# A two-layer convolution and attention kernel: folded rows in the spectra of x, packed scores, an edge row of its own, and scalings moved around the attention of layer 0

## The chip, the cores and the metric

The kernel runs on one core of a Trainium2 chip. The metric is the device time of one execution in microseconds, from the start of the program to the end of its last engine. Four compute engines work beside each other, each through its own list of instructions in order: PE (TensorE, matrix products, writes to PSUM), DVE (VectorE), ACT (ScalarE) and POOL (GpSimd). SP (SyncE) issues most DMAs.

## The reference, cut to what matters

The input `x` is 4 batches x 32 channels x 128 x 128 in float32. Layer 0 is a Fourier layer with attention over the 32 channels ("images" here), layer 1 a causal additive attention and a mixture of experts. The change touches layer 0 only.

```python
def _L0_conv_ref(x, ...):
    xn = _inorm(x.reshape(B * T, 1, H, W), norm1_w, norm1_b)
    k = _fno_layer(xn, Kcw, Ksw, Hs, Ws)      # 32 heads, at 64 x 64
    q = _fno_layer(xn, Qcw, Qsw, Hs, Ws)
    v = _fno_layer(xn, Vcw, Vsw, H, W)
    scores = jnp.einsum('bntk,bnsk->bnts', qf, kf) / sqrt(Hs * Ws)
    p_attn = softmax(scores)
    av = jnp.einsum('bnts,bnsk->bntk', p_attn, vf)
    p = _fno_layer(av, Pcw, Psw, H, W)
    a = _inorm(p + xa, attn_w, attn_b)
    an = _inorm(a, norm2_w, norm2_b)
    m = _fno_layer(an, m0cw, m0sw, H, W, inner_norm=True, act=True)
    m = _fno_layer(m, m1cw, m1sw, H, W, inner_norm=True, act=False)
    return _inorm(m, mon_w, mon_b) + a

x = x + _L0_conv_ref(_gn(x), ...)             # _gn: normed in 32 groups of columns
t = _to_tokens(x)
t = t + _L1_attn_ref(_ln_t(t), ...)
t = t + _L1_ffn_ref(_ln_t(t), ...)
```

`_fno_layer` multiplies the low Fourier modes of an image by learnt weights and adds the image times a scalar. The scores are therefore sums over modes: for keys and queries 32 rows (kx) and 17 columns (ky) carry weights for each head, all other modes of the 64 x 33 half spectrum only the scalars.

## The kernel before

**Batches and hand-overs.** Layer 0 goes through the four batches in one Python loop (`for b in range(B)`, L784), layer 1 follows. In the loop, batch `b` is mixed (attention), goes through its two mask convolutions, and near the end of its pass the spectra and the attention weights of batch `b + 1` are computed (`spectra_of_images`, `attention_weights`), so that three hand-overs stand between four batches; for batch 0 both run ahead of the loop (L696, L740). In layer 0 a scheduler sets each engine's order by the program's order and by the data; `behind(later, earlier)` adds an order by hand without a wait.

**Spectra of images** (L457 to L504). Per group of 8 images: `first_step` (L268) multiplies each image (as weights, 128 x 128) by the 128 columns `rows`, the cosines and sines of 64 kx, into `pz`. ACT copies `pz` to `z` and writes the negative of the first half behind it (L277, L278), two DVE instructions add the group's mean at kx = 0 (`shift`, L470). `forward` (L280) then makes two matmuls per image, weights `z[:, k, :P]` and `z[:, k, 64:]`, with 67 columns of `colg`, into `px` (L287, L288). DVE scales `px` by the image's inverse deviation `ysc` into `xx` (L480): partitions are (re or im, kx), columns ky. Eight DMAs write `xx` to `xd` in DRAM (L492).

**Attention weights** (L541 to L652). `xx` is copied to `xe` and `xm` (ky ahead of images) and `xe` to `xp` in PSUM. The modes without head weights (ky 17 to 32) go by matmuls into `so` (L569, 16 of them in one column group). Then 17 turns over ky: DVE and POOL multiply shifted image pairs into `pa` and `pb` (L582, L584; six buffers of tag `pr`), PE weighs them by head into `sp` and `sp0` (L597, L599). `sod` (DVE, L587) spreads `so`. ACT copies `sp` to `spt` (L601), short matmuls add all up in `sc` (L608 to L618), then maximum, difference, exponential `ex` on ACT (L625), sum, reciprocal, and `ph` on POOL (L633). `ph` goes through DRAM (`prd`, L645) into `pr` (L649), the weights of the mixing.

**Beside it, in a hand-over, batch b ends**: `spectra(1, gl, early)` (L950) makes the spectrum of the second mask convolution; `weighed` (L996) sums its energies into `v1` and `vc`, and from these some 20 small DVE steps and two pairs of Ln and Exp on ACT give the coefficients `c2`, `c3`, `cq` (L1119 to L1141). ACT scales the 32 images (`scale`, L1148), POOL adds them to `xr` in four pieces (`add_scaled`, L1158), and `back` (L339) transforms back: PE `y` (`row_products`, L321), ACT copy `v` (L335), PE `four` (L337), DVE update `last` (L1177), in two halves of 16 images. Between the halves `skip_matrix` (L654: `cm`, `cd`, `cp`, `bd`) makes the mixing matrix of the skip path. The four results go out to `x1` (L1200).

**Mixing** (L832 to L878). In blocks of 13 kx rows and 4 groups of 8 images: SP loads `xb` from `xd`, repeated over 16 heads (L841, four buffers), ACT copies it to PSUM (`xw`, L850), POOL and DVE multiply by the value weights `gb` into `u` (L859, L861), and PE sums over images with `pr` into `po` (L798); ACT copies `po` to `rs` (L878).

**Ahead of the loop**: `value_weights` (L506) computes `gd`, writes it to DRAM and reads it back as `gb`, four DMAs of 1056 KB (L531); L700 to L732 make the score weights `w_re`, `w_im` and `qk`.

## Time and profile before

| | us |
|---|---|
| median of 3 runs | 2987.97 |
| lowest and highest | 2984.72, 2988.0 |
| the profiled execution | 2987.02 |
| its span (first to last instruction) | 2985.2 |
| up to the first `po` of batch 0 | 92.4 |
| first `po` of batches 1, 2, 3 | 304.01, 510.66, 712.62 |
| layer 0 ends, layer 1's loop starts | 898 |

Busy shares over the span: PE 93%, DVE 75%, ACT 78%, POOL 69%. They are means over stages with different limits: layer 1 takes 2087 of the 2985 us, and its stretch alone has PE at 1995.9 us busy. In the hand-over from 424 to 512 us PE is busy for 80.8 us, DVE 67.9, ACT 44.2 and POOL 34.5, with DMA at 22%; in the first 93 us PE 63.2, DVE 49.9, ACT and POOL 21.0 each, with DMA at 52%. So a stage has to be read by its own chain of waits, not by the totals. A line of a timeline gives start, length, engine, line of the kernel, operation, what is written and read, and how many; in brackets, how long the engine was idle before it and what ended that. A float32 matmul appears as two records.

### The profile page before, as it was taken

Reading aid. Unit: us, or ns where it says so; the run is one execution under the profiler, and the core shown is the slowest. Engines: PE = TensorE matmul, PEld = TensorE weight load, DVE = VectorE, ACT = ScalarE, POOL = GpSimd, SP = SyncE. Lnnn points to the kernel's source line nnn. Section 1 sums busy time; section 2 is a strip of 40 time slices with the busy share of each in tenths; the row PEclk is TensorE's granted clock in tenths of the full one; section 3 lists DMA queues with packets and bytes.
Section 4 is the critical chain, followed back from the end, with each engine's and each line's share of the span. In section 5 each row is a group of like instructions: output and inputs, shape, how many; then the busy total and the mean of one; then the engine's idle time right before and its main releaser. Section 6 shows DMA issues by size and latency. Waiting matters only on the chain.

```text
span 2985.2 us, 52875 instructions
## 1 busy us (share of the span) xinstructions
PE 2779.6 (93%) x19530; PEld 1385.4 (46%) x19530; DVE 2228.6 (75%) x5024; ACT 2317.5 (78%) x3173; POOL 2057.0 (69%) x1825
## 2 busy tenths in 40 slices
PE   7789899998878999999899999999999999999997
PEld 5366565674643444443444344444444444444443
DVE  5787788788876677775678688666778766877877
ACT  2545554455358999999999999989999998999992
POOL 1704605507407897878987978898787889798773
PEclk9899999999989999999999999999999999999998
DMA  5401403304112101001010100111010020100000
GB/s 132 148 10 39 147 1 88 98 10 126 38 33 61 33 1 40 8 8 45 20 26 15 25 15 8 34 32 33 15 25 15 8 52 17 29 11 23 15 15 15
DMA packets 151731, 112.91 MB, mean 38 GB/s; under 512 B 36046, under 2 KB 139825, under 8 KB 150833
## 3 DMA queue, kind: packets, MB, share of 16 engines
q1 hardware_dynamic: 148209, 107.44, 13.6%
q8 instruction: 154, 2.52, 0.4%
q10 hardware_dynamic: 3264, 2.10, 0.2%
q14 instruction: 104, 0.85, 0.1%
HBM read 68.53 MB, written 20.00 MB: 30 GB/s over the span
## 4 chain that ended last, share of the span: by engine, by line
PE 57%; POOL 14%; ACT 10%; DVE 9%; issue 6%; DMA 1%; POOLq 0%; SPq 0%; DVEq 0%; ACTq 0%
PE d L1632 19%; PE po L1651 11%; PE px L1538 6%; ACT r L1682 5%; PE n L1632 3%; POOL e L1691 3%; POOL e L1690 3%; POOL u L859 3%; PE po L798 2%; ACT e L1698 2%; DVE r L1687 2%; POOL kx L1297 2%; POOL x L1297 1%; PE sp L597 1%; PE pz L265 1%
## 5 line engine op out<-in xcount | busy, mean ns | idle before, releaser
L1687 DVE TENSOR_TENSOR r<-n,r 128x1024 f32<-128x1024 f32 (+1 forms) x1056 | 962.0, 953 | 479.7 <-PE n L1632 390.2
L1690 POOL TENSOR_TENSOR e<-r 128x512 f32<-128x512 f32 x528 | 674.0, 1277 | 267.6 <-DVE r L1687 267.0
L1682 ACT ACTIVATE r<-d 128x1024 f32<-128x1024 f32 (+1 forms) x1056 | 793.4, 803 | 62.4 <-PE n L1632 56.1
L1694 ACT ACTIVATE r<-r 128x1536 f32<-128x1536 f32 x528 | 783.7, 1484 | 16.7
L1691 POOL TENSOR_TENSOR e<-e,r 128x512 f32<-128x512 f32 x528 | 672.3, 1273 | 41.4
L1632 PE MATMUL d<-qe,ke 32*128 32x512 f32 (+3 forms) x2304 | 605.7, 602 | 41.7 <-ACT r L1682 37.6
L1651 PE MATMUL po<-e,kx 128*128 128x512 f32 (+3 forms) x1152 | 594.3, 605 | 15.8 <-POOL e L1703 15.8
L1632 PE MATMUL n<-qe,ke 32*128 32x512 f32 (+3 forms) x2304 | 606.2, 601 | 0.0
L1632 PE MATMUL n<-qf,kf 32*128 32x512 f32 (+3 forms) x2304 | 552.6, 554 | 0.0
L1632 PE MATMUL d<-qf,kf 32*128 32x512 f32 (+3 forms) x2304 | 550.1, 553 | 0.0
L1542 DVE SCALAR_TENSOR_TENSOR xc<-px,wgt,xc 128x128 f32<-128x128 f32 x1024 | 358.3, 350 | 43.1 <-PE px L1538 10.5
L1698 ACT ACTIVATE e<-e 128x512 f32<-128x512 f32 x528 | 326.0, 617 | 67.4 <-POOL e L1691 66.6
L1651 PEld LDWEIGHTS po<-e,kx 128*128 128x128 f32 x1152 | 175.4, 188 | 393.1 <-issue 306.9
L1632 PEld LDWEIGHTS d<-qe,ke 32*128 32x128 f32 x2304 | 176.5, 183 | 361.5 <-ACT r L1682 341.0
L1632 PEld LDWEIGHTS d<-qf,kf 32*128 32x128 f32 x2304 | 220.0, 186 | 176.6 <-issue 164.2
L1538 PE MATMUL px<-we,x2t 128*128 128x512 f32 x512 | 265.9, 605 | 7.0 <-DVE xc L1542 5.8
L859 POOL TENSOR_TENSOR u<-xb,gb 128x858 f32<-128x858 f32 (+1 forms) x112 | 220.8, 2008 | 49.9 <-PE po L798 44.7
L1632 PEld LDWEIGHTS n<-qf,kf 32*128 32x128 f32 x2304 | 228.3, 185 | 18.6 <-issue 11.5
L861 DVE TENSOR_TENSOR u<-xw,gb 128x858 f32<-128x858 f32 (+1 forms) x208 | 215.7, 1109 | 20.6 <-PE po L798 9.1
L986 POOL TENSOR_TENSOR spec<-part,part 128x512 f32<-128x512 f32 x16 | 24.9, 1556 | 283.9 <-DVE part L983 130.8
L798 PE MATMUL po<-u,pr 128*32 128x429 f32 (+1 forms) x1280 | 150.5, 534 | 37.5 <-POOL u L859 21.6
L1632 PEld LDWEIGHTS n<-qe,ke 32*128 32x128 f32 x2304 | 177.8, 183 | 9.3 <-DVE r L1687 0.9
(399 smaller groups left out, 3581.0 us busy)
## 6 DMA issues: line engine op xcount, KB each, us to landing
xb<-xd SPq DMA_DIRECT2D x128, 214.5 KB
xc<-x SPq DMA_DIRECT2D x29, 512.0 KB
x<-x SPq DMA_DIRECT2D x16, 512.0 KB
qf<-qe SPq DMA_DIRECT2D x64, 128.0 KB
out<-xc SPq DMA_DIRECT2D x15, 512.0 KB
x<-in_x SPq DMA_DIRECT2D x14, 512.0 KB
xb<-xd SPq DMA_DIRECT2D x32, 198.0 KB
gb<-gd SPq DMA_DIRECT2D x4, 1056.0 KB
```

What stands on the lines that cost most here:

```text
L859: nc.gpsimd.tensor_tensor(u, xb, gk, ALU.mult)
L861: weighed_last = nc.vector.tensor_tensor(u, xw, gk, ALU.mult)
L1538: nc.tensor.matmul(px, x2t[:, k * P : (k + 1) * P], we[:, e0 : e0 + 4], start=True, stop=True)
L1542: nc.vector.scalar_tensor_tensor(xc[:, k], px[:, e], wgt[:, k, e0 + e : e0 + e + 1], xc[:, k], ALU.mult, ALU.add)
L1632: nc.tensor.matmul(o, k, q, start=turn == 0 or g > 0, stop=turn == 1 or g > 0)
L1651: nc.tensor.matmul(sums[c, h][:, q0 : q0 + c1 - c0], kx[:, jb], e[:, c0:c1], start=jb == 0, stop=is_last and q0 > 2 * P, skip_group_check= ...
L1682: nc.scalar.activation(r[:, g], d, AF.Ln, scale=1.0 / DSCALE)
L1687: nc.vector.tensor_tensor(r[:, g], part, r[:, g], ALU.mult)
L1690: nc.gpsimd.tensor_tensor(e, r[:, 1], r[:, 2], ALU.add)
L1691: nc.gpsimd.tensor_tensor(e, e, r[:, 0], ALU.add)
L1694: nc.scalar.activation(r, r, AF.Exp, scale=-1.0)
L1698: nc.scalar.activation(e, e, AF.Exp)
```

## The change

**Folded rows.** `half_rows` takes 33 cosine and 33 sine columns instead of 128 (x is real, so rows kx and -kx follow from the same two sums). The 32nd column of both goes to a small tile `z32`, the rest to `z`, 64 numbers an image; the mean is added by one ACT instruction a group. Two images at a time are the weights of one matmul with 68 columns (`columns_of`, `it`), copied to `fold` by ACT. `unfold`, once per half of the images, turns the folded sums into rows by matmuls with tables of zeros and plus or minus ones (`of_cos`, `of_sin`) on 64 partitions: one set into `em`, already in the layout of the packed scores, one set into `std`, which becomes `xx`. DVE scales both out of PSUM; ACT copies the first half of `xe` once more behind it.

**Edge row.** Row kx = 32 is computed apart (`edge_row`) and has a 65th slot in `xd`; the other rows are stored turned by 32, `xb` is read from slot 1, and the copies of `po` to `rs` turn back (one of the five is cut in two). Some DMAs change size: `kq_raw` 1088 to 576 KB, `cst` 549 to 758 KB; `xd` is written by eight DMAs after each half of the images and one for the edge row, and those for batch 0 stand ahead of three of the four `gb` loads.

**Packed attention.** The weighted modes lie on all 128 partitions, so there are 9 turns instead of 17. `so` gets 34 matmuls in four column groups, 18 of them with `hm`, a copy of `xx` masked by ACT; `sod` and `qk` have 128 partitions.

**Energies by halves.** `energy` is called for the first four slots inside `spectra(1, ...)`, for the others in `coefficients`; `weighed` takes the sums. In the hand-overs `coefficients` runs from inside `spectra_of_images`.

**Scalings around attention.** Three hooks place ACT's `scale` and POOL's `add_scaled`: 16 and two ahead of `spt`, 8 and one between `spt` and `ex`, 8 after `ex`, the last addition after `ph`. POOL's `u` is put behind that addition.

```diff
+    def half_rows(images, z, last):
+
+        for k in range(0, GI, 4):
+            pz = ps.tile([P, 4, 2, KY], F32, name="pz", tag="a")
+            for j in range(4):
+                mm = nc.tensor.matmul(
+                    pz[:, j],
+                    images[k + j],
+                    rows.rearrange("p (r x) -> p r x", r=2)[:, :, :KY],
+                    start=True,
+                    stop=True,
+                )
+            nc.scalar.copy(z[:, k : k + 4], pz[:, :, :, :32])
+            nc.scalar.copy(last[:, :, k : k + 4], pz[:, :, :, 32].rearrange("p t r -> p r t"))
+        return mm
+
...
-        steps = []
-                z = grp.tile([P, GI, 192], F32, name="z", tag="z")
-                first_step([xt[:, g + t] for t in range(GI)], z, nc.scalar.copy)
-                for k in range(2):
-                    nc.vector.tensor_scalar(
-                        z[:, :, k * P], z[:, :, k * P], shift[:, k : k + 1], None, ALU.add
...
+        def columns_of(g, z):
+
+            if g % half == 0:
+                folded[g // half] = grp.tile([P, pairs, 2 * n], F32, name="fold", tag="fold")
+            it = ps.tile([P, GI // 2, 2 * n], F32, name="it", tag="b")
+            for j in range(GI // 2):
+                mm = nc.tensor.matmul(
+                    it[:, j], z[:, 2 * j : 2 * j + 2].rearrange("p t r x -> p (t r x)"), colg[:, : 2 * n], start=True, stop=True
+                )
+                if g == GI and then is not None:
+                    behind(mm, summing["ms"])
+            k = g % half // 2
+            nc.scalar.copy(folded[g // half][:, k : k + GI // 2], it)
+        def unfold(a):
+
+            fold = folded[a]
+            t = slice(half * a, half * a + half)
+            scale = ysc[:, t].rearrange("p (k i) -> p i k", i=2)
+            em = ps.tile([P, 2, 512], F32, name="em", tag="wide")
+            em = em[:, :, : 2 * pairs * KP].rearrange("p i (m k y) -> p i m k y", m=2, y=KP)
+            for m, w in enumerate((slice(32, 96), slice(0, 64))):
+                for k, (trig, c0) in enumerate(((of_cos, n), (of_sin, 0))):
+                    for e in range(2):
+                        for i in range(2):
+                            r = slice(64 * i, 64 * i + 64)
+                            nc.tensor.matmul(
+                                em[64 * e : 64 * e + 64, i, m],
+                                trig[r, w],
+                                fold[r, :, c0 + e : c0 + e + 2 * KP : 2],
+                                start=k == 0,
+                                stop=k == 1,
+                            )
+            std = ps.tile([P, 2, 512], F32, name="std", tag="wide")
+            std = std[:, :, : pairs * n].rearrange("p i (k y) -> p i k y", y=n)
+            for i in range(2):
+                r = slice(64 * i, 64 * i + 64)
+                nc.tensor.matmul(std[:, i], of_cos[r, 96:], fold[r, :, n:], start=True, stop=False)
+            for i in range(2):
+                r = slice(64 * i, 64 * i + 64)
+                nc.tensor.matmul(std[:, i, :, :KY], of_sin[r, 96:], fold[r, :, :KY], start=False, stop=True)
+            for m, dst in enumerate((xe, xm)):
+                nc.vector.tensor_tensor(
+                    dst[:, :, t].rearrange("p y (k i) -> p i k y", i=2),
+                    em[:, :, m],
+                    scale.unsqueeze(3).to_broadcast([P, 2, pairs, KP]),
+                    ALU.mult,
+                )
...
+            if a == 0:
+                nc.scalar.copy(xe[:, :, T:], xe[:, :, t])
+            nc.vector.tensor_tensor(
+                xx[:, t].rearrange("p (k i) y -> p i k y", i=2),
+                std,
+                scale.unsqueeze(3).to_broadcast([P, 2, pairs, n]),
+                ALU.mult,
+            )
+            nc.vector.tensor_copy(xx[:1, t, 0], bias)
+            for part in range(2):
+                for x0 in (32, 0):
+                    nc.sync.dma_start(
+                        out=xd[t, part, 32 - x0 : KX - x0].rearrange("t x y -> x t y"),
+                        in_=xx[KX * part + x0 : KX * part + x0 + 32, t, :KY],
...
-            forward(z, colg[:, 0], colg[:, 1], scaled)
...
+        def edge_row():
+
+            m = 2 * n - 1
+            o32 = ps.tile([m, T], F32, name="o32", tag="a")
+            nc.tensor.matmul(o32, colg[:, n:], z32[:, 0], start=True, stop=False)
+            nc.tensor.matmul(o32, colg[:, :m], z32[:, 1], start=False, stop=True)
...
+            nc.tensor.matmul(t32, x32, ident[:m, :m], start=True, stop=True)
...
+            nc.scalar.copy(s32[:, :m], t32)
+            nc.sync.dma_start(
+                out=xd[:, :, KX], in_=s32.rearrange("t (r y) -> t r y", r=2)[:, :, :KY]
+            )
+            return x32, w32
+
+        waiting = []
+        for g in GROUPS:
+            z = grp.tile([P, GI, 2, 32], F32, name="z", tag="z")
+            made = half_rows([xt[:, g + t] for t in range(GI)], z, z32[:, :, g : g + GI])
+            if g == 0:
+                ysc, scaled = image_weights(sv, made)
+            if g == GI and then is not None:
+                then(made)
+            nc.scalar.activation(z[:, :, 0, 0], z[:, :, 0, 0], AF.Identity, bias=shift)
+            if waiting:
+                columns_of(*waiting.pop())
+            if g == 3 * GI:
+                unfold(0)
+            waiting.append((g, z))
+        columns_of(*waiting.pop())
+        edges = edge_row()
+        unfold(1)
+        return xx, (xe, xm), xd, edges, ysc
...
+        xp = ps.tile([P, KP, T + half], F32, name="xp", tag="wide")
+        copied = nc.scalar.copy(xp, xe)
+        masked = 2 * KP
+        hm = modes.tile([P, T, masked], F32, name=f"hm_{b}", tag="hm")
+        nc.scalar.activation(hm[:, :, 1:], xx[:, :, 1:masked], AF.Identity, scale=high)
+        copied = nc.scalar.activation(hm[:, :, 0], xx[:, :, 0], AF.Identity, scale=half_high)
...
+        same_time = [(xx[:, :, yy], xx[:, :, yy]) for yy in range(masked, 32)]
+        same_time += [(w32, x32), (xh, xs)]
+        same_time += [(hm[:, :, yy], xx[:, :, yy]) for yy in range(masked)]
+        for k, (wt, moved) in enumerate(same_time):
             nc.tensor.matmul(
-                so, x_y, x_y.unsqueeze(1).to_broadcast(twice), start=yy == KA, stop=False
+                so[32 * (k % 4) : 32 * (k % 4) + 32],
+                wt,
+                moved.unsqueeze(1).to_broadcast([moved.shape[0], 2, T]),
+                start=k < 4,
+                stop=k >= len(same_time) - 4,
             )
...
-        for yy in range(KA):
-            row = xp[:, yy // 9, yy % 9 * (T + half) :]
+        for yy in range(KP):
+            row = xp[:, yy]
...
         spt = grp.tile([P, 2, T, half], F32, name="spt", tag="pr", bufs=6)
-        nc.scalar.copy(spt, sp.unsqueeze(1).to_broadcast([P, 2, T, half]))
+        ahead = hooks[0](copied, on_pool) if hooks else None
+        act = nc.scalar.copy(spt, sp.unsqueeze(1).to_broadcast([P, 2, T, half]))
+        if ahead is not None:
+            behind(act, ahead)
+        ahead = hooks[1](act) if hooks else None
...
+        if ahead is not None:
+            behind(softmax, ahead[0])
...
-            nc.gpsimd.tensor_tensor(
+            product = nc.gpsimd.tensor_tensor(
...
+            if ahead is not None:
+                behind(product, ahead[1])
+        if hooks:
+            hooks[2](softmax, product)
...
-                        in_=xd[8 * i : 8 * i + 8, r, x0 : x0 + nk]
+                        in_=xd[8 * i : 8 * i + 8, r, 1 + x0 : 1 + x0 + nk]
...
-                            nc.gpsimd.tensor_tensor(u, xb, gk, ALU.mult)
+                            weighed = nc.gpsimd.tensor_tensor(u, xb, gk, ALU.mult)
+                            if "added" in roots:
+                                behind(weighed, roots["added"])
...
-            nc.scalar.copy(rs[:, x0 : x0 + nk].rearrange("p x y -> p (x y)"), po)
+            cut = min(max(KX // 2 - 1 - x0, 0), nk)
+            for lo, hi, to in ((0, cut, x0 + KX // 2 + 1), (cut, nk, x0 + cut - KX // 2 + 1)):
+                if lo < hi:
+                    nc.scalar.copy(
+                        rs[:, to : to + hi - lo].rearrange("p x y -> p (x y)"), po[:, lo * KY : hi * KY]
+                    )
...
@@ -947,7 +1054,21 @@
 
             nc.scalar.activation(spec[:, slots, :64], spec[:, slots, P:], AF.Copy, scale=-1.0)
 
-        def spectra(layer, src, ready=()):
+        def energy(s, sq, by_row, slots, earlier=None):
+
+            n = slots.stop - slots.start
+            t = sq[:, 1, slots]
+            product = nc.vector.tensor_tensor(
+                t.rearrange("p t (r x) -> p t r x", r=2),
+                sq[:, 0, slots].rearrange("p t (r x) -> p t r x", r=2),
+                by_row.unsqueeze(1).unsqueeze(1).to_broadcast([P, n, 2, KX]),
+                ALU.mult,
+            )
+            if earlier is not None:
+                behind(product, earlier)
+            nc.vector.tensor_reduce(s[:, slots], t, AX.X, ALU.add)
+
+        def spectra(layer, src, ready=(), weights=(), earlier=None):
 
             by_re, by_im = layers[layer][:2]
             spec = big.tile([P, GI, 192], F32, name="spec", tag="spec")
@@ -974,6 +1095,9 @@
                 nc.scalar.activation(
                     sq[:, 0, s4], px.rearrange("p t r x -> p t (r x)"), AF.Square
                 )
+                if a == 0:
+                    for t, by_row in weights:
+                        energy(t, sq, by_row, s4, earlier)
                 one_, two = (
                     grp.tile(shape, F32, name=n, tag="v", bufs=3) for n in ("part1", "part2")
                 )
@@ -993,21 +1117,12 @@
                     negative(spec, s4)
...
+        sums_of = [small.tile([P, GI], F32, name=n, tag=n) for n in ("v1_r", "vc_r")]
+        spec, sq = spectra(
+            1,
+            gl,
+            early,
+            [(t, w[0]) for t, w in zip(sums_of, layers[1][2:4])],
+            normed[4] if b + 1 < B else None,
+        )
+        made = {}
+
+        def coefficients(product=None):
+
+            for t, w in zip(sums_of, layers[1][2:4]):
+                energy(t, sq, w[0], slice(4, GI))
+            tag = "a" if product is None else "wide"
+            v1 = weighed("v1", sq, squares, layers[1][2], tag, sums_of[0], product)
+            vc = weighed("vc", sq, squares, layers[1][3], tag, sums_of[1], product)
+            r1, _ = inv_std("r1", v1)
...
-            weights = attention_weights(b + 1, front)
-            for t in range(T):
-                behind(scale(t), weights[5])
-            for i in images_of:
-                behind(add_scaled(i), weights[6])
+            def first_half(copied, on_pool):
+
+                for t in range(T // 2):
+                    act = scale(t)
+                    behind(act, copied)
+                for i in images_of[:2]:
+                    behind(add_scaled(i), on_pool)
+                return act
+
+            def third_quarter(scores):
+
+                for t in range(T // 2, 3 * T // 4):
+                    act = scale(t)
+                    behind(act, scores)
+                return act, add_scaled(images_of[2])
+
+            def rest(softmax, product):
+
+                for t in range(3 * T // 4, T):
+                    behind(scale(t), softmax)
+                roots["added"] = add_scaled(images_of[3])
+                behind(roots["added"], product)
+
+            weights = attention_weights(b + 1, front, (first_half, third_quarter, rest))
```

## The prediction, made before the changed kernel ran

> **What bounds the kernel now.** I read the page's slices first (layer 0 ends near 898 us, where the line L1632 of layer 1 takes over; no line that the change touches runs later), then the chain of waits over layer 0, then the timelines of PE, ACT and POOL around one hand-over between batches (424 to 512 us), and last the timelines of SP and PE for the first 100 us.
>
> The chain of waits in the hand-over from batch 1 to batch 2 (start, us, what):
>
> ```profile
> 442.66 1.97 PE pz L276 x16
> ...
> 465.50 0.24 PE px L288 x2
> 465.76 0.45 DVE xx L480
> 466.25 3.67 PE so L569 x30
> ...
> 488.25 1.00 ACT spt L601
> ...
> 499.12 1.07 DVE x L1177 x4
> ...
> 510.66 0.92 PE po L798 x4
> ```
>
> Nothing else useful runs in these 68 us: PE first works without a gap through `pz` and `px` (442.5 to 465.7, 23.2 us), then the score products take until 488.25, then a chain of small steps until the next batch's first `po`. The other two hand-overs have the same shape (`spt` at 281.62 and 693.37, first `po` at 304.01 and 712.62). So a microsecond removed here is one removed from the end, until another engine is late.
>
> ACT and POOL in that hand-over (timeline: start, length, engine, what, idle before):
>
> ```profile
> 469.52 12.43 ACT L1148 ACTIVATE g<-g,cq,c 128x128 f32<-128x128 f32 x32 [0.28 <-DVE cq L1141]
> 492.43 1.06 ACT L625 ACTIVATE ex<-less 64x1024 f32<-64x1024 f32 x1 [3.19 <-DVE less L623]
> 493.39 1.52 ACT L335 COPY v<-y 128x512 f32<-128x512 f32 x3
> ...
> 487.04 9.29 POOL L1158 TENSOR_TENSOR x<-x,g 128x1024 f32<-128x1024 f32 x4
> 496.30 3.12 POOL L633 TENSOR_TENSOR ph<-ex,sm 32x512 f32<-32x512 f32 x2
> ```
>
> SP and PE in the first batch (same columns):
>
> ```profile
> 60.14 20.74 SPq L841 DMA_DIRECT2D xb<-xd  x8
> 81.24 6.12 SPq L645 DMA_DIRECT2D prd<-ph  x4
> ...
> 92.40 1.66 PE L798 MATMUL po<-u,pr 128*32 128x429 f32 x8 [9.53 <-DMA xb<-xd]
> 95.74 4.42 PE L798 MATMUL po<-u,pr 128*32 128x429 f32 x24 [1.69 <-DMA pr<-prd]
> ```
>
> ACT has a hole for 12.4 us of scalings only while the scores are long. POOL's four additions push `ph` about 1.8 us (the softmax sum's reciprocal ends at 494.5, `ph` starts at 496.3). In the first batch `ph` is done at 80.7, and PE still waits until 92.4 for DMAs: SP spent 20.7 us on eight `xb` issues ahead of `prd`.
>
> [...] with full 128x128 weights a record of 128 columns takes 0.122 us (`pz`, 0.97 us for 8) and one of 67 columns still 0.112 us (`px`, 0.22 us for 2). So halving the columns saves little, halving the number of matmuls saves half. [...] The trace shows four-way packing of 32-wide tiles (`px` L972: 16 records of up to 256 columns in 0.99 us), no 64x64 one. [...]
>
> **The change, part by part,** for one hand-over, on the clock of 1 to 2. Where I name an order after the change, it is that in which the changed program's instructions stand on each engine.
>
> PE's front. Removed: `pz` 64 records x 0.122 = 7.8 us and `px` 128 x 0.112 = 14.3 us, 22.1 in all. Added: `pz` of 66 columns, 64 x 0.112 = 7.2; `it`, 16 matmuls for two images each, 32 x 0.112 = 3.6; the edge row, some 0.5; two unfoldings. An unfolding is 16 matmuls 64x64 of 72 columns (32 records) and 4 of 272 columns (8 records). Below: packed four ways at the 0.034 us a record that the row-packed `y` L321 shows (1.83 us for 54), and the 8 at half of 0.26 us (272/512 of `four`'s 0.495): 2.2 us. Above: 32 x 0.112 + 8 x 0.26 = 5.7 us. I take 3.0, near the packed end, since consecutive matmuls go to different tiles; two are 6.0. Sum 17.3, so 4.8 us less.
>
> Behind the front: today `xx`, two bias copies, `xe`, `xm` and `xp` follow the last `px`, 3.7 us until the first `pa` (469.40). After, `xe` and `xm` leave PSUM directly and only one `xp` copy follows (some 1.9 us after the last `em`); `std` of the second half (1.5 us of PE) and xx's eviction lie beside that. Gain 1.8 + 1.5, and two early `pz` give 0.5. First `pa` at 469.4 - 4.8 - 1.8 - 1.5 - 0.5 = 460.8.
>
> Scores. The loop falls from 17 to 9 turns. VectorE now does 17 `pa` and 5 `pb` x 0.635 and `sod` 1.1, 15.1 us of the 18.9 between first `pa` and `spt`; after, 9 + 3, 7.6 and 1.1, and between them xx's second half, `xs`, `xh` (1.3 us). `so` grows to 34 matmuls but in four column groups: 68 records x 0.045 (between `px` L972's 0.062 and `y`'s 0.034) = 3.1 instead of 3.9. But it now needs the masked copy `hm` (1.2 us on ACT, as `xm` cost) after xx, so the first `sp` comes some 4 us after the first `pa`, not 1. I take 3 us for this delay and 1.0 more for waits on buffers: 7.6 + 1.1 + 1.3 + 3 + 1.0 less 0.3 of overlap is 13.7, `spt` at 474.5, 13.75 us earlier. Bounds: 12 (delay hidden) to 16.
>
> Tail. `spt` to `ex` takes 4.2 us; eight scalings x 0.388 = 3.1 fit in the 3.19 of idleness there. POOL: pb ends near 471, three additions x 2.3 = 6.9 lie before `ph`; the third needs scalings that end near 478.7 and ends at 481; `ph` starts there, about when the reciprocal is ready (480.8). So `ph` no longer waits for the fourth. But the last eight scalings stand on ACT between `ex` and the copies `v` L335 (behind them: `four`, 16 updates `x` L1177, then `cd`, since VectorE's order keeps these updates first). That is +3.1 us: `ex` 478.7 to 479.8, scalings to 482.9, first `x` at 484.7 (now 495.24), `cd` at 489.7 (now 500.24). From `cd` to the first `u` VectorE is busy as before (8.4 us, 508.6 to be compared with 498.1). Net 10.5 us a hand-over: the 1.8 won at `ph` is not needed, since `cd` waits for VectorE. Bounds: if ACT's order costs nothing, 13.7; if the unfoldings cost 5.7 each and the delays run full, 6.5.
>
> Three hand-overs: 31.5 us (19.5 to 41).
>
> First batch. `gd` is written out some 4 us earlier (VectorE's list puts the value weights before the image work), the xb issues move behind `prd` and the first `pr`, and the spectra and scores end earlier: `ph` near 64 by the same steps. Then DMA is late: the four `gb` loads, 4.3 MB, took from 37.7 until about 79.5 with the `xd` beside them (8 issues now, 9 after), at 106 to 138 GB/s in the table of stretches, and that is no shorter. They start near 34.5, the last lands near 76.5; `pr` and the first `xb` follow, `u`, and `po` near 81.5. Against 92.40 that is 11, and the 2 us that the second step waits for `pr` go too: 13 us. Below: 5 (loads overlap worse, since three `gb` are issued only after the last `xd`); above: 20 (the loads were held by issue, not by bandwidth). Constants: cst grows by 210 KB, under 1 us at the 300 GB/s of these first stretches, kq_raw shrinks by 512 KB; called even.
>
> Last batch. Here the coefficients are the path: the full energies run 866.60 to 871.72 on VectorE (2 x 1.22 + 2 x 1.21 and small ones). Half of that now lies in VectorE's idle time before: 2.4 us (0 to 3).
>
> At nothing: the split copy of `rs` (one more ACT instruction a batch, ACT is idle before it; 0.3 us if not), the waits of POOL's `u` behind the last addition (ends near 487, before `po` can start), energies by halves in the hand-overs (done at 448, wanted after 460; without that cover 0.5 us), the SP issues of eight `xd` and one edge row (before `prd`, which waits for `ph` anyway).
>
> Sum: 31.5 + 13 + 2.4 = 46.9. The profiled execution took 2987.0 (span 2985.2 and 1.8 around it); 2987.0 - 46.9 = 2940.1. The median shown, 2988.0, is 1.0 above it, no more than the runs differ.
>
> **Rivals.**
> 1. Forecast, 2940: front and scores shorter, scalings on ACT and loads of `gb` give some back. 0.60.
> 2. Full gain: unfoldings pack ideally and the tail is not held by ACT. 3 x 14 + 18 + 2.4 = 62: 2925. For it: `cm` is ready early, and PE has slack in the tail. Against: the orders of ACT and VectorE are fixed. 0.20.
> 3. DMA and the start of the scores keep most: 3 x 6.5 + 4 + 1 = 25: 2962. For it: the 9.53 us wait for `xb`. Against: PE's front is counted matmul by matmul. 0.15.
> 4. Slower: the 64x64 matmuls do not overlap at all and each record takes its whole length (0.28 us as `px`, 0.45 for the long ones): 64 x 0.28 + 16 x 0.45 = 25 us instead of 6 in each hand-over. Then 3 x (19 - 10.5) = 25 lost, the first batch even, 2.4 won: 3010. It decides from 0.2 us a record over the 80 (16.5 us for both unfoldings). Against it: every packed group in the trace is far below. 0.03.
> 5. The gains are all hidden by something unseen: 2987. 0.02.
>
> **Numbers.** The predicted time is the forecast's, 2940. Its own bounds (19.5 to 41, 5 to 20, 0 to 3, and 2 us of layer 1's own spread) and most of rivals 2 and 3 give 2921 to 2961; outside stay rivals 4 and 5 and parts of 2 and 3, under 2 in 10. Within 0.2% (6 us, about what a measurement can tell) is 0.02, slower 0.03, faster 0.95.
>
> **What would show it.** In the profile after: both unfoldings about 6 us of PE (wrong step if 9 or more); `spt` some 32 us after the last `px` of the mask convolution instead of 46; eight ACT scalings between `ex` and `v`, with first `po` some 25.5 us after `spt` instead of 22.4; the first `po` of batch 0 near 81 after a DMA wait; layer 1 still 2087 us. If `po` follows `spt` as fast as now, the tail term was wrong; if the first `po` stays at 92, the `gb` term.

## The result, and the profile after

| | before | after | forecast |
|---|---|---|---|
| median of 7 runs each, us | 2988.0 | 2977.4 | 2940 (range 2921 to 2961) |
| profiled execution / its span | 2987.0 / 2985.2 | 2975.9 / 2974.2 | 2940.1 |
| ratio after to before, 95% interval | | 0.9967 [0.9956, 0.9979] | 0.984 |
| first `po` of batch 0 | 92.40 | 88.28 | 81.5 |
| layer 1's loop starts | 898.99 | 887.36 | 852 |

The change makes the kernel faster, but by about 11 us instead of 47. Layer 1 takes 2086.2 us before and 2086.8 after, so all of it happens in layer 0. I read a hand-over in stages, each from an event in the timelines to the next; the forecast column is the prediction's own working for the hand-over from batch 1 to 2, the others are means over the three hand-overs of the profiled execution:

| stage of a hand-over, us | before | forecast | after |
|---|---|---|---|
| last gelu ends → last `px` of the mask convolution ends | 11.2 | 11.5 | 18.1 |
| → first `pa` | 27.1 | 18.5 | 18.3 |
| → `spt` | 18.3 | 13.7 | 12.9 |
| → first `v` copy | 5.2 | 8.4 | 8.2 |
| → first `u` on VectorE | 15.2 | 15.2 | 17.5 |
| sum | 77.0 | 67.3 | 75.0 |

Two rows carry the miss, the first and the last. The second and third, where the folded rows and the packed scores are, came out as forecast or better. The chain of waits of the changed kernel in the hand-over from batch 1 to 2 shows both places:

```profile
427.67 0.68 DVE part L1104
...
429.31 1.17 DVE gn_r L255
...
431.01 0.69 PE bg L380 x2
...
478.79 3.17 ACT g L1283 x8
481.96 0.48 ACT v L357
```

Before the change the chain ran from the mask convolution on PE into `pz` of the front without VectorE's small group-scale steps in it. Now `gn_r` and `bg` stand on it, and at its end the eight scalings `g` ahead of `v`. PE's timeline of the kernel before, at the same two places:

```profile
440.87 0.43 PE L358 MATMUL bg<-both,ones 128*128 128x64 f32 x2
441.24 1.06 PE L972 MATMUL px<-z,cst 128*32 128x256 f32 x20
...
494.01 1.98 PE L337 MATMUL four<-v,cst 128*128 128x512 f32 x4 [1.35 <-ACT v L335]
```

And of the changed kernel:

```profile
431.01 0.69 PE L380 MATMUL bg<-both,ones 128*128 128x64 f32 x2 [3.49 <-DVE both L446]
431.49 3.73 PE L305 MATMUL pz<-cst,g 128*128 128x128 f32 x16
...
453.22 0.82 PE L521 MATMUL em<-fold,cst 64*64 64x72 f32 x32
453.97 0.73 PE L532 MATMUL std<-fold,cst 64*128 64x272 f32 x4
454.53 0.61 PE L535 MATMUL std<-fold,cst 64*128 64x264 f32 x4
...
482.48 3.78 PE L359 MATMUL four<-v,cst 128*128 128x512 f32 x4 [4.37 <-ACT v L357]
```

The reader should see three things. Two holes, 3.49 and 4.37 us. After each, PE's records take twice as long: `pz` 3.73/16 = 0.23 us where the same line takes 0.12 elsewhere, `four` 3.78/4 = 0.95 where the kernel before took 1.98/4 = 0.50. I call this half clock: the tables of stretches show a granted clock of 0.50 for 430 to 434 us and 1.00 for 438 to 442. And an unfolding (`em` and `std`) costs 2.2 us, the lower bound of the prediction, not the 3.0 that I took.

The first batch, in the chain of waits of the changed kernel:

```profile
68.05 1.50 POOL ph L732
...
71.15 8.66 DMA prd<-ph
...
79.95 0.39 SPq L752
```

`ph` starts at 68 and ends at 71, and was forecast near 64; the 32 KB writes of `prd` need 8.66 us to land, and only then is `pr` issued (SP, L752). The gain up to the first `po` is 4.1 us of the forecast 10.9, and it is an uncertain 4.1: in six executions of programs whose first batch no edit touches (the changed kernel and the first, second, third, fourth and eleventh run below), the first `po` came at 88.3, 86.2, 92.6, 88.4, 86.4 and 92.9. Part of this spread is the clock: in the two late ones (runs 2 and 11) it was still 0.50 from 46 to 50 us, where the other four had 1.00, and `ph` ended 2 us later.

### The profile page after: what moved, and what is told of

The parts are those of the page before. It is cut to its first block, busy times and chain, and to the rows that moved or that the text cites. A ratio compares the mean times of both kernels' runs of the same rounds, so it can differ in the third digit from the quotient of the medians.

```text
span 2974.2 us, 52576 instructions
## 1 busy us (share of the span) xinstructions
PE 2741.9 (92%) x19442; PEld 1356.0 (46%) x19442; DVE 2189.5 (74%) x4934; ACT 2314.2 (78%) x3217; POOL 2031.1 (68%) x1801
## 4 chain that ended last, share of the span: by engine, by line
PE 60%; POOL 13%; ACT 11%; DVE 9%; issue 6%; DMA 1%; SPq 0%; POOLq 0%; DVEq 0%; ACTq 0%
PE d L1786 20%; PE po L1805 12%; PE px L1692 6%; ACT r L1836 5%; PE n L1786 4%; POOL e L1845 3%; POOL e L1844 3%; PE po L898 3%; POOL u L959 2%; ACT e L1852 2%; PE pz L305 2%; POOL kx L1451 2%; DVE r L1841 1%; PE px L1093 1%; DVE xc L1696 1%
## 5 line engine op out<-in xcount | busy, mean ns | idle before, releaser
L1852 ACT ACTIVATE e<-e 128x512 f32<-128x512 f32 x528 | 326.4, 618 | 67.3 <-POOL e L1845 66.3
L1786 PEld LDWEIGHTS n<-qf,kf 32*128 32x128 f32 x2304 | 228.5, 186 | 19.5 <-issue 11.5
```

The costliest lines, as they stand in the source:

```text
L1786: nc.tensor.matmul(o, k, q, start=turn == 0 or g > 0, stop=turn == 1 or g > 0)
L1852: nc.scalar.activation(e, e, AF.Exp)
```

## Experiments

Runs 1 to 3 and 11 are the changed kernel with the edit shown. Run 4 joins runs 1 and 2, runs 5 to 9 add one edit each to run 4 (run 8 two), and runs 10 and 12 add one to run 9. Times are medians; the ratio is to the kernel before, run beside it on the same chip (its median was 2983 to 2986 us there).

### Run 1: group scales behind the mask convolution again

```diff
-        if b + 1 < B:
-            normed = image_scales(*summed)
...
+        if b + 1 < B:
+            normed = image_scales(*summed)
+            for t, w in zip(sums_of, layers[1][2:4]):
+                energy(t, sq, w[0], slice(0, 4), normed[4])
```

> The changed kernel with one part undone: the group scales of the next batch (the chain gn_r, both, colg and the matmul bg) stand again behind the second mask convolution in the program, as before the change; the first halves of the energies follow them. Theory A (the order ahead of the front): in the changed kernel the last px of the mask convolution ends 19.0 us after the last gelu (before: 11.6), because PE stands behind bg for 3.5 us and then runs at half clock. Here it ends 11.5 to 13 us after it, the first pa comes 6 to 7 us earlier in every hand-over, and the time is 2956 to 2960 us. Rival A1 (only the half clock costs, the wait would come anyway): 2 to 3 us a hand-over, 2968 to 2972. Rival A2 (the front waits for the group scales, colg and my, so moving them back only moves the wait): less than 1 us a hand-over, 2974 to 2979.

Measured: 2959.65 us, ratio 0.9918 [0.9901, 0.9934]; against the changed kernel's 0.9967 that is 15 us. PE's timeline of this run:

```profile
425.51 0.63 PE L1093 MATMUL px<-z,cst 128*32 128x256 f32 x4
426.06 0.44 PE L380 MATMUL bg<-both,ones 128*128 128x64 f32 x2
426.43 1.06 PE L1093 MATMUL px<-z,cst 128*32 128x256 f32 x20
```

`bg` now stands between two groups of `px`, with no hole before it. From the gelu to the last `px` takes 10.9 us (after: 18.1, before: 11.2). Theory A holds for the place and the 7 us, and both rivals fall. But the first `pa` is only 5 us nearer to the gelu, because the next stage, the front of the next batch, grew from 18.3 to 20.4. Two things are in that. The clock now falls to half for 3.4 us inside each of the three fronts. And PE's order has changed: two matmuls of `pz` no longer stand ahead of the last `px`, and PE waits for the energies:

```profile
437.90 0.41 PE L380 MATMUL ms<-vc_s,ones 128*128 128x32 f32 x2 [0.54 <-DVE vc_s L1134]
```

In two later fronts with this order and no fall of the clock (one each of runs 6 and 8) the stage takes 19.4, so the order is worth about 1.1 us and the clock 1.0.

### Run 2: no scaling after the exponential

```diff
-                for t in range(T // 2):
+                for t in range(3 * T // 4):
-                for t in range(T // 2, 3 * T // 4):
+                for t in range(3 * T // 4, T):
-                for t in range(3 * T // 4, T):
-                    behind(scale(t), softmax)
```

> The changed kernel with the ACT scalings split 24 ahead of spt, 8 between spt and ex, none after ex (changed kernel: 16, 8, 8). Theory B (the tail): the last eight scalings hold the copies v for 3.1 us, PE then idles 4.4 us and runs four at half clock; without them v comes 3.1 us earlier, PE idles about 1.3 us and keeps its clock, and the first u of the second step comes 5 us earlier in every hand-over: 2961 to 2965 us. Rival B1 (as my prediction had it, cd waits for VectorE and nothing but the 3.1 us itself is there): 3 us a hand-over, 2968 to 2970. Rival B2 (ph and the loads of pr are late, so nothing is won): 2975 to 2979. If the eight scalings ahead of spt do not fit, spt comes up to 1 us later.

Measured: 2962.16 us, ratio 0.9921 [0.9898, 0.9944], as theory B has it. PE's timeline of this run:

```profile
478.64 1.99 PE L359 MATMUL four<-v,cst 128*128 128x512 f32 x4 [1.52 <-ACT v L357]
```

The hole is 1.52 us, and `four` runs at 0.50 us a record. `spt` to `v` is 5.1 us and `v` to `u` 15.5, in all three hand-overs: 5.1 us won each time: 3.1 ahead of `v`, where the scalings stood, and 2.0 behind it, where `four` and its followers no longer run at half clock. The 24 scalings ahead of `spt` end at 472.0, 0.9 us before it.

### Run 3: the same holes, filled with spare matmuls

```diff
+    def keep_busy(tile, times):
+        for _ in range(times):
+            nc.tensor.matmul(tile, rows, cst[:, :512], start=True, stop=True)
...
+            keep_busy(ps.tile([P, 512], F32, name="busy", tag="a"), 4)
         nc.vector.tensor_copy(by_group, sums("bg", ones, both, "a"))
...
         four = ps.tile([P, 4, C], F32, name="four", tag=tag)
+        keep_busy(four, busy)
```

Four of them are put ahead of `bg`, four ahead of the first `four` of a hand-over (`busy` is 4 there, else 0).

> The changed kernel with its order and waits as they are, and four spare matmuls of 512 columns (results overwritten) put on PE in each of two holes of a hand-over: ahead of bg, and ahead of the first four after the scores. Theory C (half of the loss is the clock that falls after a hole): pz behind bg at 0.12 us a record instead of 0.23 (1.8 us), the first fours at 0.5 instead of 0.95 us a record (about 2.3 us); up to 4 us a hand-over, 2964 to 2969 us. Rival C1 (the wait itself is the loss, and what runs at half clock lies beside other waits): within 1 us a hand-over, 2974 to 2978. Rival C2 (the spare matmuls run at half clock themselves and push bg and four): slower, 2979 to 2985.

Measured: 2974.26 us, ratio 0.9966 [0.9953, 0.9979]: no difference to the changed kernel, and by its total alone a point for rival C1. The stages say otherwise. In the first place it worked: gelu to last `px` fell from 18.1 to 14.9 us, with `bg` still ahead of the second half of the mask convolution (PE's order moved a little: one group of `px` now stands behind `bg`). In the second the spare work did not stay where it was meant to be. PE's timeline of this run:

```profile
466.52 1.13 PE L381 MATMUL four<-cst 128*128 128x512 f32 x2
467.58 1.05 PE L700 MATMUL sp<-pb,w_im 128*32 128x512 f32 x2
468.55 1.13 PE L381 MATMUL four<-cst 128*128 128x512 f32 x2
```

Two of the four stand among the score products `sp`, ahead of `spt`, and the stage from `pa` to `spt` grew from 12.9 to 16.2 us: 2.1 us are the two spare matmuls, and the clock fell beside them (0.70 for 456 to 460 us, 1.00 in the changed kernel). The other two stayed in the hole and left 2.45 us of it; `v` to the first `u` took 16.4 instead of 17.5. So the clock, with what little moved on PE, gives back 3.2 of the 6.9 us lost ahead of the front; how much of the rest is pure waiting was not separated further.

### Run 4: runs 1 and 2 together

> The edits of the first two runs together: group scales behind the mask convolution, and no scaling after ex. Theories A and B are independent places on one chain, so the gains add: 11 to 12 us a hand-over, 2941 to 2946 us, which is close to what my prediction gave for the hand-overs alone. Rival D (the second wait hides part of the first, or another engine is late in the tail): 2950 to 2958.

Measured: 2951.57 us, ratio 0.9886 [0.9872, 0.9901]. The gains add less than fully, which is the number of rival D, though not by its mechanism: the tail is as short as in run 2 (`spt` to `u` 20.9 us) and the part ahead of the front as in run 1 (11.2), but the front between them takes 21.6 us (20.4, 22.3, 22.0), where run 1 took 20.4 and the changed kernel 18.3. The table of stretches of this run (stretch, length, then busy time of PE, PEld, DVE, ACT and POOL, granted clock, DMA share, GB/s) shows why:

```profile
430.50:434.50 4.00, 3.47 (x32) 3.33 (x30) 1.67 (x7) 2.32 (x11) 0.00 (x0) 1.00 0.02 4
434.50:438.50 4.00, 3.46 (x26) 3.24 (x24) 3.17 (x21) 1.53 (x7) 0.00 (x0) 0.85 0.00 0
438.50:442.50 4.00, 4.00 (x45) 2.94 (x44) 2.21 (x11) 1.15 (x5) 0.00 (x0) 0.50 0.00 0
```

The clock falls to half while PE is busy for 3.5 us of every 4. It was at half for 3.4, 10.4 and 6.8 us of the three fronts. In the changed kernel the clock stands at 1.00 in all of its fronts. There it was at half behind the hole (0.50 for 430 to 434 us) and at full again just ahead of the front (1.00 from 438 on), with the 128-column `pz` L305 in between. That its fronts kept the clock because of this is my reading; no run tries it.

### Run 5: all 128 columns in the first batch's rows

On top of run 4, for batch 0 only; the copies take the same 66 columns as before.

```diff
+            nx = KX if wide else KY
-            pz = ps.tile([P, 4, 2, KY], F32, name="pz", tag="a")
+            pz = ps.tile([P, 4, 2, nx], F32, name="pz", tag="a")
-                    rows.rearrange("p (r x) -> p r x", r=2)[:, :, :KY],
+                    rows.rearrange("p (r x) -> p r x", r=2)[:, :, :nx],
```

> The kernel of the fourth run (both orders) with one more edit: in the first batch alone, half_rows multiplies by all 128 columns again instead of 66, and the copies take the 66 they need. In the changed kernel PE's front of the first batch runs from 22.0 to 46 us without a hole and yet at half clock (pz 0.227 us a record, it 0.24) until the long matmuls of std; before the change the 128-column pz reached full clock after 8 us. Theory E (matmuls of 66 columns do not count as enough work to raise a clock that is down): the records of pz fall to 0.12 us after some 5 us, the first pa comes at 40 to 42 us instead of 49.2, and the three late gb loads are issued at 43 to 45 instead of 52.7. po then comes about 6 us earlier (80 to 82 instead of 86.4): 2944 to 2947 us against 2951.6. Rival E1 (the clock rose at 44 us for another reason; width plays no part): pa within 1 us of 49, the time within 2 us of 2951.6. Rival E2 (pa moves, but gb's loads set po whatever the front does): pa at 41, po within 2 us of 86.4, the time the same.

PE's timeline of the changed kernel, and then of this run:

```profile
22.02 3.63 PE L290 MATMUL pz<-cst,x 128*128 128x66 f32 x16
...
29.65 5.33 PE L290 MATMUL pz<-cst,x 128*128 128x66 f32 x24
```

```profile
22.26 3.39 PE L291 MATMUL pz<-cst,x 128*128 128x128 f32 x16
...
28.91 2.00 PE L291 MATMUL pz<-cst,x 128*128 128x128 f32 x16
```

Twice the columns, and the record falls from 0.21 to 0.125 us (the granted clock is 1.00 from 26 us on), while with 66 columns PE works from 22 to 44 us with no hole above 0.3 us and stays at 0.22. The first `pa` comes at 40.6 instead of 49.2: theory E holds for the clock and E1 falls. But `po` stays at 86.1, as rival E2 said. The time is 2948.12 us, ratio 0.9879 [0.9862, 0.9895], not distinguishable from run 4.

### Run 6: three spare matmuls ahead of the first front

```diff
+        if first:
+            keep_busy(ps.tile([P, 512], F32, name="busy", tag="a"), 3)
         nc.vector.tensor_copy(by_group, sums("bg", ones, both, "a"))
```

> The kernel of the fourth run with three spare matmuls of 512 columns on PE in the hole between the moments and bg of the first batch (17.8 to 21.6 us), pz with 66 columns as in the change. Theory E with a memory: the hand-overs keep full clock through 66-column matmuls once it is up (0.11 to 0.12 us a record between 440 and 455 us), so here pz starts at 0.12 and keeps it, the first pa comes at 38 to 40 us, po at 80 or earlier: 2943 to 2946 us. Rival E3 (66-column matmuls lose the clock again within some us even where it was up): pz falls back to 0.23 a record before 30 us and pa is at 46 or later, the time within 2 us of 2951.6.

PE's timeline of this run:

```profile
19.25 1.96 PE L379 MATMUL busy<-cst 128*128 128x512 f32 x4
...
22.28 1.95 PE L290 MATMUL pz<-cst,x 128*128 128x66 f32 x16
```

With the clock up at the start the same 66-column records take 0.12 us, and the first `pa` comes at 39.5. The clock held over this front (1.00 in every stretch from 22 to 54 us), so rival E3 falls; run 4 shows that it does not always hold. `po` is again at 86.0, not at 80 or earlier; 2947.28 us, ratio 0.9878 [0.9863, 0.9893].

### Runs 7 and 8: the loads of gb ahead of xd, without and with the wide rows

```diff
-    front = spectra_of_images(0, loaded, normed)
     value_weights()
+    front = spectra_of_images(0, loaded, normed)
```

> The kernel of the fourth run with the value weights ahead of the first batch's spectra in the program, so that all four gb loads are issued behind gd and ahead of the xd writes (the changed kernel issues one at 36 us and three at 52.7 to 55.7, behind the last xd). Theory F (the first po is set by the last gb load, and that by its issue): gb lands some 12 us earlier, and the first po follows pr (prd at 69.7, pr some 10 us later) near 80 instead of 86.4: 2944 to 2947 us. Rival F1 (the loads share one queue and xb and xd stand behind gb, so po stays): po 85 to 88, the time within 2 us of 2951.6. Rival F2 (VectorE does the value weights ahead of the scaling of the spectra and delays pa): pa 2 to 4 us later, the time 2951 to 2955.

> The fourth run's kernel with both edits of the first batch: 128 columns in half_rows for batch 0, and gb ahead of xd. If theories E and F hold, spectra and scores end 8 us earlier (ph near 61 instead of 69) and gb no longer waits for xd, so po comes near 74 to 77 us: 2939 to 2943 us. If the gb loads alone are the bound (4.3 MB at the 110 to 150 GB/s that the stretches show, from 36 us on: 65 to 75 us), po comes near 78 to 80 and the time is 2943 to 2946. If neither matters, 2950 to 2953.

Measured: 2945.79 us, ratio 0.9872 [0.9858, 0.9887], and 2944.48 us, 0.9868 [0.9845, 0.9891], with the first `po` at 86.5 and 86.7. Theory F falls as I put it: the four loads are issued from 29 to 33 us in run 8 instead of up to 56, `ph` is ready by 64, and `po` does not move, as rival F1 said. (In run 7 the first `pa` comes 2.8 us later, as F2 had it, and that does not move `po` either.) SP shows what happens instead: in run 8 its first four `xd` issues take 27.3 us, while `gb` is being moved; in the changed kernel they took 3.2.

### Run 9: the wide rows in every batch

> The fourth run's kernel (both orders) with all 128 columns in half_rows for every batch. In the fourth run the clock falls to half between 437 and 450 us, in the middle of the front (66-column pz, 68-column it, 72-column em), with PE busy 3.5 of every 4 us; in the run with spare matmuls in the first batch it stayed up in the same place. Theory E (narrow matmuls count as too little work, not only to raise the clock but to hold it): with 128 columns the clock stays up, gelu to first pa takes 30.5 to 31.5 us in all three hand-overs (fourth run: 31.9, 33.2, 33.1), 0.5 us of it for the wider records; in the first batch the first pa comes at 41. Time 2944 to 2948 us against 2951.6. Rival E4 (the fall comes from waits of PE on ACT's copies, not from the width): the half clock stays where it is and the front is 0.5 us longer per hand-over, 2951 to 2954.

Measured: 2938.23 us, ratio 0.9843 [0.9828, 0.9858]. The table of stretches of this run, the front of the same hand-over:

```profile
426.00:430.00 4.00, 3.78 (x35) 3.63 (x33) 2.84 (x9) 2.58 (x11) 0.40 (x1) 1.00 0.01 4
430.00:434.00 4.00, 3.97 (x36) 3.78 (x35) 3.46 (x21) 2.11 (x10) 0.00 (x0) 1.00 0.00 0
434.00:438.00 4.00, 3.76 (x58) 3.07 (x57) 3.02 (x17) 2.00 (x8) 0.00 (x0) 1.00 0.00 0
```

Clock 1.00 throughout. Last `px` to first `pa` is 18.4 to 18.5 us in all three hand-overs (run 4: 21.6 on average), and the time is below theory E's 2944 to 2948. The wide rows are not faster record for record (0.121 us, and 0.118 for 66 columns at full clock in run 4); the front is shorter because the clock stays up, and not by that alone: PE's order changed with the width, and PE no longer waits for `vc_s`. Against the two narrow fronts that kept the clock, 19.4 us, the wide ones win 0.9; so some 2.2 of the 3.1 us belong to the clock. Rival E4 falls by its number, but since the waits changed with the width, these two runs do not separate them fully. A batch now takes 191.7 us from inverse to inverse; it took 206.8 before the change and 204.6 after it.

### Run 10: gb on ACT's queue

```diff
-                read = nc.sync.dma_start(
+                nc.scalar.dma_start(
                     out=gb[:, k, ri],
```

> The kernel of the run before with the four gb loads issued by ACT instead of SP, so that prd, pr, xd and xb do not stand in the same queue behind gb's 4.3 MB. In the four runs that moved the first batch's front or the gb issues, the first po stayed at 86.0 to 86.7 us although ph was ready between 61 and 72: SP is held in xd or prd (12 to 27 us for four issues) and pr is only issued at 78.4 to 79.1. Theory F3 (the queue's order: all stand behind gb's data): pr is in place by 70, po follows the last needed gb load and comes at 72 to 78: 2936 to 2942 us. Rival F4 (the bytes: gb's own data lands near 76 to 80 on whatever queue): po at 80 to 84, 2941 to 2946. Rival F5 (ACT is held by the issues as SP was, and the copies behind them with it): first pa later than 45, po 86 or more, 2947 to 2955.

Measured: 2940.91 us, ratio 0.9851 [0.9835, 0.9868]; first `po` at 94.5. SP's timeline of this run:

```profile
37.35 21.30 SPq L558 DMA_DIRECT2D xd<-xx  x4
...
69.66 6.16 SPq L558 DMA_DIRECT2D xd<-xx  x4
76.20 7.45 SPq L940 DMA_DIRECT2D xb<-xd  x8
83.75 5.39 SPq L747 DMA_DIRECT2D prd<-ph  x4
```

Nothing of `gb` is in this queue any more, and the small `xd` writes still take until 75.8. Theory F3 falls: it is not the order within one queue that holds them. F5 falls too (first `pa` at 42.8). `po` is later than F4 has it and than in run 9 because SP's order also put eight `xb` ahead of `prd`, so this run does not test F4's number.

### Run 11: the last batch's energies undivided

```diff
-            [(t, w[0]) for t, w in zip(sums_of, layers[1][2:4])],
+            [(t, w[0]) for t, w in zip(sums_of, layers[1][2:4])] if b + 1 < B else (),
-                energy(t, sq, w[0], slice(4, GI))
+                energy(t, sq, w[0], slice(4 if b + 1 < B else 0, GI))
```

> The changed kernel with the energies of the last batch undivided, as before the change. My prediction gave the division 2.4 us there. The traces say: from the last square of px to the coefficients cq the changed kernel takes 14.45 us and the kernel before 15.3, while the earlier half stands ahead of the product part on VectorE and the last square comes 0.7 us later than it would. Theory G (the division nets almost nothing): from the last gelu to layer 1's first d 50.6 to 51.1 us (changed kernel 50.77, before 50.9), the time within its scatter of 2977. Rival G1 (as predicted): 2 to 2.5 us longer, 52.8 to 53.3.

Measured: one execution, 2981.4 us, which by itself tells nothing (its first `po` was one of the two late ones); last gelu to layer 1's first `d` is 53.4 us (changed kernel 50.8, before 50.9), so near G1's number and not G's. It does not read that simply, though. From the end of the last square to the input of the first inverse root (`r_ve` L247) takes 7.6 us here, 5.8 in the changed kernel and 6.8 before: the division is worth 1.8 us at its own place. But the last square itself comes 0.7 us earlier here, and behind the root a copy `v` stands at another place in VectorE's order (0.6 us) and another copy `v` ahead of the logarithm in ACT's (1.4 us), which the edit did not ask for. What the division nets is read below.

### Run 12: gb in five pieces

On top of run 9: only the rows that the first block of the mixing needs are read ahead, the others one block ahead of their use.

```diff
+    gd, written = value_weights()
+    load_weights(gd, 0, written)
...
+                if b == 0 and i == 1 and x0 + NK < KX:
+                    load_weights(gd, x0 + NK, broadcast)
```

> The ninth run's kernel (both orders, 128 columns in half_rows) with each gb load cut into the five blocks of rows that the mixing uses: only the first block (0.86 of 4.3 MB) is read ahead of the first batch's xd, each later block is issued with the xb loads of the block before it. In six runs the first po of batch 0 stayed between 86.0 and 88.0 us, whatever was done to the front, to the place of gb's issues, and (94 us) with gb on another queue. Theory F6 (it is gb's bytes: prd, pr and xb can only be moved once 4.3 MB are through): prd leaves at 62, pr and xb are in place by 68 to 70, the first po comes at 68 to 74, the inverse of batch 0 starts at 130 to 138 instead of 148.6: 2922 to 2930 us against 2938.2. Rival F7 (the same bytes are then moved beside xb, whose loads set the pace of the mixing): po at 68 to 74 too, but the mixing of batch 0 takes 70 us instead of 60, the inverse starts at 141 to 147: 2932 to 2938. Rival F8 (bytes are not it; the first xb or pr is slow by itself): po at 84 or later, 2937 to 2941.

Measured: 2920.0 us, ratio 0.9779 [0.9763, 0.9796]. PE's and SP's timelines of this run:

```profile
61.62 2.96 SPq L754 DMA_DIRECT2D prd<-ph  x4
65.77 0.39 SPq L758 DMA_DIRECT2D pr<-prd  x1
```

```profile
67.85 1.66 PE L905 MATMUL po<-u,pr 128*32 128x429 f32 x8 [2.55 <-DMA pr<-prd]
```

`prd` lands in 4 us, `po` comes at 67.9 (in the changed kernel 8.66 and 88.3), and the inverse of batch 0 starts at 132.7 instead of 148.6. The mixing takes 64.9 us instead of 60.6, so F7's contention is there, but small. Theory F6 holds (the time is 2 us below its range): what kept the first `po` at 86 to 88 was 4.3 MB that had to be moved first. This version is faster than both kernels.

## Why the prediction was wrong

In the profiled executions the change gained 11.0 us of span: 5.2 up to the inverse of batch 0 (forecast 13), 6.7 over the three batches that follow (31.5), a loss of 0.3 in the last (2.4), and 0.6 lost in layer 1.

**The hand-overs.** Each was forecast at 10.5 us and gave 2.0 by the stages above, and the failure lies in two steps.

The first is one that the prediction does not have. It starts its sum at the end of the mask convolution ("PE's front. Removed: ...") and takes that end as given. The change also moves `image_scales(*summed)` from behind `spectra(1, ...)` to ahead of it, which the description of the change does not name; in PE's order that puts `bg` ahead of the second half of the mask convolution, and `bg` waits for seven small VectorE steps, which themselves stand among the products `part`. The prediction thus has its cost at nothing, without a reason. It was 6.9 us a hand-over, shown by run 1: undone, the stage is 10.9 us again (a whole hand-over then gains 5.7, since the front behind it grows by 2.1). None of the signs that the prediction said to watch lies in this stage: `spt` came 31.1 us after the last `px` (32 forecast), and the eight scalings stood where it said.

The second is the tail. The forecast has "+3.1 us: `ex` 478.7 to 479.8, scalings to 482.9", and `v` did come 8.2 us after `spt` (8.4 by that line). What the step left out is that PE, with nothing to do for 4.4 us, comes back at half clock (0.50 for 482 to 486 us): `v` to the first `u` took 17.5 us and not 15.2. Run 2 removes both and gives 15.5. The term, 3.1 us, was mis-sized by 2.1: it is 5.1.

The steps that were worked out matmul by matmul held. Last `px` to first `pa` was to fall by 8.6 us and fell by 8.8; the scores were to give 5.15 and gave 5.4. In the first of these some luck is mixed in: the two unfoldings took 4.7 us of PE and not 6.0, and two holes of 0.31 and 0.53 us that the sum does not have, with records of 0.118 us where it has 0.112, ate the difference. With the two orders mended and the clock kept up (run 9), the five stages take 62.6 us instead of 77.0, 14.4 less; the forecast without the tail's cost has 13.7. That run 9's 2938 us lies next to the forecast's 2940 is luck: its hand-overs gain more than forecast and its first batch less.

**The clock.** The changed kernel's trace shows a granted clock of 0.50 behind both holes of the hand-over: for 430 to 434 us behind the one of 3.49 us, for 482 to 486 us behind the one of 4.37 us, with records twice as long after each. Behind the hole of 1.35 us at the same place in the kernel before it was 1.00 (494 to 502 us). Nor was it enough that PE was busy: it worked 22 us at half clock with 66-column matmuls (changed kernel, 22 to 44 us), and fell to half within such work (0.85 and 0.50 in run 4's table, with PE busy for 3.5 and 4.0 of 4 us). The prediction took its spacing of records, 0.112 and 0.122 us, from a stretch at full clock (1.00 from 442 to 466 us before the change) and carried it to every front. The first batch's front, for which it claimed earlier spectra "by the same steps", ran at half clock (0.50 from 22 to 42 us), and `ph` ended at 71 instead of 64; with the clock up (run 6) it ended at 61.6.

**The first batch.** The prediction named the right bound, the four loads of `gb`, and its sign. The failing term is "`pr` and the first `xb` follow, `u`, and `po` near 81.5", five us after a last load landing "near 76.5". In the changed kernel `pr` was issued at 79.95, once `prd` had taken its 8.66 us, and `po` followed 8.3 us later. In runs 5 to 9 `pr` was only issued between 78.4 and 80.3 and `po` followed 7.6 to 7.8 us later, whether the last load was issued at 33 or at 60 us and whether `ph` was ready at 62 or at 74. The order within one queue is not the reason for the wait: run 10 shows the same hold-up with `gb` on another queue. The six equal first batches above spread over 6.7 us, so that a single profile could not have settled it. Run 12 shows the cause by taking it away.

**The last batch.** Between the last gelu and the coefficients `cq` the kernel before takes 32.0 us and the changed one 31.8. By comparison with run 11: dividing the energies gives 1.8 us (forecast 2.4), the first half's work ahead of the product `part` takes 0.7 back, the new order of the two sums around the first root a net 0.4, and a copy `v` L227 that now falls between `dq` and `cg` on VectorE, and before fell into a wait, 0.6. The term was 0.6 us too large, and the step "Half of that now lies in VectorE's idle time before" was not checked for what stands behind it. These last three are differences of the traces and were not tried one by one.

**The rivals.** None was it. The time lies between rivals 3 and 5, and rival 5 ("hidden by something unseen", 0.02) comes nearest in kind: three quarters of the gain were hidden, most of it in a stage that no rival names. Rival 2 fell with the tail, which ACT did hold. Rival 3 (DMA and the start of the scores keep most, 2962) had the right sign and half of the cause in the first batch; the scores started as forecast. Rival 4 fell at once: a record of an unfolding takes 0.03 to 0.18 us, tail included.

## What to carry to other kernels

Follow a moved line on each engine's own order: what matters is not what it computes but which instructions queue behind its first waiting one. A gain that is cut out of PE can come back as a hole, and the holes of 3.5 and 4.4 us were paid twice here, once as a wait and once as half a clock. Before trusting an idle stretch of an engine as cover, read what stands behind it in that engine's order. Where a transfer of megabytes stands between a program's start and its first product, ask first which part of it that product needs.

## What the hardware showed that I had not expected

Matmuls with few moving columns did not raise PE's clock from half, and did not always keep it up. With 128x128 weights, 66 columns and no holes above 0.3 us, a record took 0.22 us for 22 us on end; with 128 columns it fell from 0.21 to 0.125 us (clock 1.00 from 26 us on in run 5, from 30 in run 9). Where the clock was up it could survive 15 us of narrow work (run 6, the first batch) or fall to 0.50 in its middle (run 4). Of the eighteen narrow fronts of runs 1 and 4 to 8, sixteen stood at half clock for 3.4 to 11.8 us and took 20.4 to 23.0 us, and two kept the clock and took 19.4; the nine wide ones of runs 9, 10 and 12 all kept it and took 18.4 to 18.5. But the nine narrow fronts of the changed kernel and of runs 2 and 11, which follow the half clock of the hole, kept it too. Multiplying twice the needed columns, at 0.121 us a record instead of 0.118, won 3.1 us a hand-over on average (2.0 to 3.8, runs 4 and 9), of which about 0.9 goes with PE's changed order. Whether it is the number of moved columns, or something that goes with them, these runs do not tell.

The bytes of one load held back small writes of another queue: with `gb` issued by ACT, four `xd` writes of 66 KB still held SP for 21.3 us (2.2 in run 12, where one fifth of `gb` goes ahead of them).
